# Layer 3 of a graph network on one core: two transfers of SyncE change places in each period

## The chip, the core and the metric

The kernel runs on one NeuronCore of a Trainium2 chip. Its engines work side by side, each on its own queue of instructions in the order in which they were written: PE (TensorE, matmuls; its weight loads are shown as PEld), DVE (VectorE), ACT (ScalarE), POOL (GpSimd) and SP (SyncE, which here only issues DMA transfers; ACT issues a few as well). Engines wait for one another by semaphores. The metric is the device time of one execution in microseconds (us): 2101.37 us for the kernel before, the median of three runs from 2099.18 to 2102.93.

## The reference, cut to what is computed

Four graph layers follow one another, each on `x + layer(relu(layernorm(x)))` with x of 32 graphs x 512 nodes x 64 features and one 512 x 512 adjacency matrix. The change lies in layer 3, a graph attention with 8 heads and then an output attention:

```python
def gat_layer(x, graph, W, b):
    h = x @ W
    s = jnp.einsum('bnd,bmd->bnm', h, h) * graph
    s = jnp.where(s == 0.0, NEG_INF, s)
    a = jax.nn.softmax(s, axis=2)
    return jnp.einsum('bnm,bmd->bnd', a, h) + b
heads = jax.vmap(lambda W, b: gat_layer(flow_x, graph, W, b))(Wh, bh)
...
x = jax.nn.leaky_relu(cat, negative_slope=0.01)
out = gat_layer(x, graph, W_out, b_out)
return jax.nn.leaky_relu(out, negative_slope=0.01)
```

Each softmax needs a maximum and a sum for every row of scores. Since the scores are symmetric, the kernel works on the transposed matrix: the maximum that it finds along one partition has to be subtracted along a column, so it must reach all partitions.

## The kernel before

Layers 0 to 2 take the first 450 us or so. Layer 3 then runs as 144 units: 128 pairs of attention heads (class `Heads`, L474) and 16 output attentions for two graphs each (class `Out`, L585). A unit has four row blocks r = 0 to 3 of 128 rows (C = 4), and each block holds two 512-column halves. A unit goes through these steps:

- `scores(r)`, L365: PE, two matmuls a block into a PSUM tile `s_ps`. That pool has two buffers (L1260), and `e_ps` of `exps` comes from the same two.
- `maxima(r)`, L375: DVE, two custom instructions a block (L382); they take the scores with the mask into `p_att` and leave the row maxima in `top`.
- `spread_out()`, L387: DVE transposes `top` (L389), and SP writes it into a small DRAM tile `top_row` with four transfers of 1 KB (L392).
- `spread_in()`, L396: SP reads `top_row` back, broadcast to all partitions, into `topb`, 128 x 1024 values, 512 KB (L398). This is the "broadcast of the maxima's rows". It must wait until `top_row` has landed.
- `shift(r)`, L403: POOL subtracts `topb` from a block (L404).
- `exps(r)`, L409: ACT takes the exponential of a block (L413), for odd r into `e_ps`. `join(r)`, L415: DVE adds block r - 1 to odd block r (L416).
- `totals()`, L429: PE sums the rows (L434), and ACT copies the result to `tot` (L439).
- `totals_out()`, L441: the sums are brought into a narrow form, `parts`, by two transfers of 4 KB, one issued by SP and one by ACT (both L446). SP's is the "spreading transfer of the sums". It must wait for the copy `tot`.
- `recips()`, L450: DVE adds the two parts (L452) and inverts them (L455). `recips_out()`, L457, and `recips_in()`, L463: SP sends them through DRAM (L459, L466) to `recb`.
- `values(j)`, L418: PE multiplies with the features (L422). `normalize()`, L470: DVE multiplies with `recb` (L472).
- `y_pe` (L549), `y_act` (L559) and `y_dve` (L568) of `Heads`: PE, ACT (L563) and DVE (L571) make the head's output `cat`. `Out` has `y_act` (L638), `back`, `back_dve`, `back_pool` and `store` (L641 to L663) in their place.

The order is written by hand. `planned` (L703) returns `period(t)`, and the loop at the end of layer 3 calls it once for each t. In period t, `now` is unit t, `ahead` is unit t + 1, and `unit(k)` is unit t - k. So one period works on several units at once: maxima of unit t, shifts and exponentials of unit t - 1, sums and values of unit t - 2, normalizing of unit t - 3, and the head output of unit t - 4. All five engines are under a manual schedule, so that each engine's instructions stand in its queue exactly as the calls in `period` follow one another. Two orders matter below:

- on ACT: `exps(0)` of unit t - 1, then `y_act` of unit t - 4, then `exps(2)`, the copy `tot` of unit t - 2, ACT's transfer of the sums, `exps(1)` and `exps(3)`;
- on SP: `recips_in` of unit t - 3, the four transfers of `spread_out` and the broadcast of `spread_in` (unit t), then SP's transfer of the sums (unit t - 2), `recips_out` (unit t - 2) and, where unit t - 5 is an `Out`, `store`.

PSUM tiles of the pool `ps_m` have two buffers (L1261) shared by `y_ps`, `tot_ps`, `back_ps` and a few others: in an ordinary period `totals` takes the buffer that the first half of `y_dve` has just read.

Of the kernel before, what the change touches and what calls it, by code (L numbers as in the profile page):

```python
# [22 lines left out]
def fast_form(  # L23
# [645 lines left out]
    def any_zero():  # L669

        def across(src, rows, name):
            ps = ps_m.tile([P, P], F32, name=name, tag="m")
            n = src.shape[0]
            nc.tensor.transpose(ps[:rows, :n], src, ident[:n, :n])
            return ps[:rows, :n]

        own = tiny.tile([P, 1], F32, name="own")
        nc.vector.tensor_reduce(own, least, AX.X, OP.min)
        two = tiny.tile([1, 2], F32, name="two")
        nc.vector.tensor_reduce(two[:, 0:1], across(own, 1, "own_ps"), AX.X, OP.min)  # L680
        best = tiny.tile([B // 2, 2], F32, name="best")
        nc.vector.tensor_reduce(
            best,
            across(least_out, B // 2, "out_ps").rearrange("b (k f) -> b k f", k=2),
            AX.X, OP.max,
        )
        worst = tiny.tile([B // 2, 1], F32, name="worst")
        nc.vector.tensor_reduce(worst, best, AX.X, OP.min)
        nc.vector.tensor_reduce(
            two[:, 1:2], across(worst, 1, "worst_ps"), AX.X, OP.min  # L690
        )
        flag = tiny.tile([1, 1], F32, name="flag")
        nc.vector.tensor_reduce(flag, two, AX.X, OP.min)
        nc.vector.scalar_tensor_tensor(
            again, flag, 0.0, unsound, op0=OP.is_equal, op1=OP.max
        )
# [6 lines left out]
    def planned(units, products):  # L703

        class Nothing:
            def __getattr__(self, name):
                return lambda *args: None

        nothing = Nothing()

        def period(t):
            def unit(lag):
                return units[t - lag] if 0 <= t - lag < len(units) else nothing

            now, ahead = unit(0), unit(-1)
            for r in range(2, C):
                now.scores(r)
            unit(3).recips_in()
            unit(4).y_pe()
            unit(1).shift(0)  # L720
            unit(1).exps(0)
            unit(4).y_act()
            u, h = products.get(t - 1, (None, 0))
            if u and h == H - 1:
                u.keep_product()
            unit(1).shift(2)
            unit(1).exps(2)
            for r in range(2, C):
                now.maxima(r)
            now.spread_out()  # L730
            now.spread_in()
            for r in range(2):
                ahead.scores(r)
            unit(4).y_dve()
            unit(3).normalize()
            for r in range(2):
                ahead.maxima(r)
            unit(4).back()
            unit(2).totals()
            unit(2).totals_out()  # L740
            unit(1).shift(1)
            unit(1).exps(1)
            u, h = products.get(t, (None, 0))
            if u:
                u.product(h)
            for j in range(C):
                unit(2).values(j)
            unit(1).join(1)
            unit(1).shift(3)
            unit(1).exps(3)  # L750
            unit(5).back_pool()
            unit(-2).make_gs()
            unit(2).recips()
            unit(2).recips_out()
            unit(5).store()
            unit(4).back_dve()
            unit(1).join(3)
            unit(-3).features(3)
            unit(-2).judge_product()
            unit(1).make_v()  # L760
            unit(-4).make_hx()
            unit(-2).make_g()
            for step in range(3):
                for lag, odd in ((step - 7, 0), (step - 11, 1)):
                    u = unit(lag)
                    if getattr(u, "i", None) == 0 and u.b % 2 == odd:
                        u.features(step)
            if t == len(units):
                any_zero()

        return period
# [1067 lines left out]
```

## Time and profile before

| What | before |
|---|---|
| runs (median, lowest, highest) | 2101.37, 2099.18, 2102.93 us |
| profiled execution: own time / span of its profile | 2099.58 / 2097.8 us |
| busy in the span: PE, DVE, ACT, POOL | 2002.6, 1786.2, 1227.9, 1432.7 us |
| starts of the copies `tot` (L439), first and last of 144 | 484.4 and 2075.8 us |
| mean distance of two such copies | 11.13 us |
| SP's issue: broadcast L398 / sums L446 | 0.35 / 0.57 us each |

The profile's page gives busy times of each engine, the costliest groups of instructions and what ended the idle time before them. The other views used are the waits (who waited for whom: us in total, times, longest), and the timeline of a window, in which each row is: start and length in us, engine, line, operation, tiles written and read, and in brackets the engine's idle time before it and what ended that. SPq and ACTq are transfers issued from the sequencers of SP and ACT; the length of such a row is the time that the issuing takes and not the flight of the data. The packet records of the trace give each DMA packet's start, length, size and queue; packets of SP's transfers are on queue 1, of ACT's on queue 10. The distance from one copy `tot` to the next is used as the length of a period.

### The profile page before, as it was taken

What the parts mean: (1) busy time and instruction counts of PE and PEld (TensorE: products, weight loads), DVE (VectorE), ACT (ScalarE), POOL (GpSimd) and SP (SyncE); (2) the same over time, 40 slices, a digit from 0 to 9 for tenths busy, and PEclk for the clock granted to TensorE, in tenths of its full rate; (3) what the DMA queues carried; (4) which work ended last, traced back from release to release, by engine and by line L of the source; (5) the groups of instructions that cost most, each with busy time, mean ns of one, the idle gap of its engine ahead of it and who ended that gap; (6) DMA issues with size and microseconds to landing.
All of it is one profiled execution on the core that took longest, in us unless ns stands there. A gap on an engine that the chain in (4) does not pass through costs nothing. (4 is left out here: it accounts for less than half of the span.)

```text
span 2097.8 us, 33009 instructions
## 1 busy us (share of the span) xinstructions
PE 2002.6 (95%) x11038; PEld 813.8 (39%) x11038; DVE 1786.2 (85%) x4257; ACT 1227.9 (59%) x1944; POOL 1432.7 (68%) x697
## 2 busy tenths in 40 slices
PE   7999999988999999999999999999999999999995
PEld 4667676652333333333333333333333333333321
DVE  6699997667998989898989898989888888988983
ACT  3444443335666666666666666666666666766553
POOL 3000000018898889888888988888888888888995
PEclk9999999989999999999999999999999999999998
DMA  5000000001222222222222222222222222222222
GB/s 139 1 1 2 1 2 1 1 22 57 77 75 69 78 77 73 78 76 82 68 78 77 72 77 77 77 71 74 68 77 73 77 67 73 77 71 74 77 68 78
DMA packets 135780, 129.35 MB, mean 62 GB/s; under 512 B 92792, under 2 KB 98080, under 8 KB 135472
## 3 DMA queue, kind: packets, MB, share of 16 engines
q1 hardware_dynamic: 116368, 126.35, 19.8%
q10 hardware_dynamic: 18720, 0.59, 0.5%
q8 instruction: 89, 1.46, 0.3%
q0 software_dynamic: 512, 0.20, 0.1%
q14 instruction: 91, 0.75, 0.1%
HBM read 119.48 MB, written 5.37 MB: 60 GB/s over the span
## 5 line engine op out<-in xcount | busy, mean ns | idle before, releaser
L404 POOL TENSOR_TENSOR p_att<-p_att,topb 128x1024 f32<-128x1024 f32 x576 | 1347.4, 2374 | 232.7 <-DMA topb<-top_row 130.6
L382 DVE CUSTOM_DVE_ANT_0 p_att<-s_ps,flow_neg 128x512 f32<-128x512 f32 x1152 | 727.8, 685 | 53.6 <-PE s_ps L370 51.9
L370 PE MATMUL s_ps<-hx,g 64*128 64x512 f32 x2048 | 545.3, 615 | 34.3 <-DVE p_att L416 24.6
L413 ACT ACTIVATE e_ps<-p_att 128x1024 f32<-128x1024 f32 x288 | 295.8, 1028 | 174.2 <-DVE top L382 107.8
L413 ACT ACTIVATE p_att<-p_att 128x1024 f32<-128x1024 f32 x288 | 304.2, 1056 | 149.6 <-POOL p_att L404 146.6
L416 DVE TENSOR_TENSOR p_att<-e_ps,p_att 128x1024 f32<-128x1024 f32 x288 | 346.5, 1203 | 24.7 <-ACT e_ps L413 24.4
L370 PEld LDWEIGHTS s_ps<-hx,g 64*128 64x128 f32 x2048 | 179.4, 186 | 343.1 <-DVE top L382 163.2
L422 PE MATMUL av<-p_att,hd 128*64 128x512 f32 x1024 | 264.3, 593 | 2.2 <-DVE o_att L472 2.0
L422 PE MATMUL av<-p_att,hn 128*64 128x512 f32 x1024 | 263.7, 592 | 0.0
L1053 POOL TENSOR_TENSOR x<-x,bias_b 128x512 f32<-128x512 f32 x16 | 20.3, 1271 | 280.0 <-DVE hn L826 280.0
L571 DVE SCALAR_TENSOR_TENSOR cat<-y_ps,bh,cat 128x512 f32<-128x512 f32 x256 | 178.1, 737 | 6.2 <-ACT cat L563 3.4
L563 ACT ACTIVATE cat<-y_ps,bh 128x512 f32<-128x512 f32 x256 | 161.7, 680 | 11.8 <-PE y_ps L553 8.7
L434 PE MATMUL tot_ps<-p_att,ones 128*32 128x512 f32 x1152 | 154.8, 610 | 1.6 <-DVE cat L571 0.5
L553 PE MATMUL y_ps<-o_att,wh_sb 64*128 64x512 f32 x512 | 143.2, 589 | 0.0
L598 PE MATMUL gT_ps<-cat,wo_sb 128*64 128x512 f32 x512 | 138.1, 618 | 0.0
L439 ACT COPY tot<-tot_ps 128x512 f32<-128x512 f32 x144 | 84.4, 586 | 85.0 <-PE tot_ps L434 83.6
L422 PEld LDWEIGHTS av<-p_att,hd 128*64 128x64 f32 x1024 | 73.2, 137 | 152.2 <-issue 141.2
L422 PEld LDWEIGHTS av<-p_att,hn 128*64 128x64 f32 x1024 | 74.8, 137 | 144.9 <-issue 144.9
L472 DVE TENSOR_TENSOR o_att<-av,recb 128x512 f32<-128x512 f32 x144 | 98.3, 683 | 34.9 <-DMA recb<-rec_row 34.6
L547 ACT COPY g<-g_ps 128x512 f32<-128x512 f32 x128 | 70.3, 588 | 95.3 <-PE g_ps L535 95.3
L977 PE MATMUL acc<-v,s 64*128 64x65 f32 x2048 | 124.1, 280 | 0.7 <-DVE s L963 0.4
L977 PEld LDWEIGHTS acc<-v,s 64*128 64x128 f32 x2048 | 121.2, 195 | 5.9 <-DVE o L993 1.2
(181 smaller groups left out, 2028.2 us busy)
## 6 DMA issues: line engine op xcount, KB each, us to landing
topb<-top_row SPq DMA_DIRECT2D x144, 512.0 KB
recb<-rec_row SPq DMA_DIRECT2D x288, 128.0 KB
top_row<-top_t SPq DMA_DIRECT2D x576, 1.0 KB
out_dram<-y SPq DMA_DIRECT2D x32, 128.0 KB
x<-in_x_dram SPq DMA_DIRECT2D x3, 1024.0 KB
parts<-tot ACTq DMA_DIRECT2D x144, 4.0 KB
parts<-tot SPq DMA_DIRECT2D x144, 4.0 KB
rec_row<-rec_flow SPq DMA_DIRECT2D x144, 4.0 KB
```

Source lines behind the costliest of these rows:

```text
L370: nc.tensor.matmul(ps[:, k], lhsT=g[halves(k), r * P : (r + 1) * P], rhs=x[halves(k), :], start=True, stop=True,)
L382: nc.vector.tensor_tensor_reduce(out=self.p[r][:, k], in0=ps[:, k], in1=flow_neg[:, r], scale=-1.0, scalar=BIG, op0=OP.add, op1=OP.min, ac ...
L404: nc.gpsimd.tensor_tensor(self.p[r], self.p[r], self.topb, OP.subtract)
L413: nc.scalar.activation(to, self.p[r], AF.Exp, scale=-1.0)
L416: nc.vector.tensor_tensor(self.p[r], self.joined, self.p[r - 1], OP.add)
L422: nc.tensor.matmul(self.av[halves(k), :], lhsT=self.v(k, j) if j % 2 else self.less_next(k, j), rhs=self.p[j][:, k], start=(j == 0), stop= ...
L434: nc.tensor.matmul(ps[q : q + 32, :], lhsT=ones, rhs=self.p[2 * e + 1][:, k], start=True, stop=True,)
L553: nc.tensor.matmul(ps, lhsT=wh_sb[halves(k), 2 * self.i + k, :], rhs=self.o[halves(k), :], start=True, stop=True,)
L563: nc.scalar.activation(self.cat[:, k], self.y[k], AF.Identity, bias=bh01[:, h : h + 1], scale=0.01)
L571: nc.vector.scalar_tensor_tensor(self.cat[:, k], self.y[k], bh[:, h : h + 1], self.cat[:, k], op0=OP.add, op1=OP.max,)
L598: nc.tensor.matmul(self.gps[halves(k), :], lhsT=wo_sb[:, h, :], rhs=Heads.cat.pop((self.b + k, h)), start=(h == 0), stop=(h == H - 1),)
L977: nc.tensor.matmul(self.acc[k][:, r], lhsT=self.s[b // 2][halves(k), b % 2, r * P : (r + 1) * P], rhs=self.v[halves(k), b], start=(b == 0) ...
```

## The change

In `period`, the call `now.spread_in()` moves from directly behind `now.spread_out()` to behind `unit(2).totals_out()`. Only SP's queue changes: in each period the broadcast L398 of unit t now stands behind SP's transfer of the sums L446 of unit t - 2, and no longer ahead of it. The instructions of PE, DVE, ACT and POOL are the same in the same order, and nothing is added or removed.

```diff
             for r in range(2, C):
                 now.maxima(r)
             now.spread_out()
-            now.spread_in()
             for r in range(2):
                 ahead.scores(r)
             unit(4).y_dve()
...
             unit(4).back()
             unit(2).totals()
             unit(2).totals_out()
+            now.spread_in()
             unit(1).shift(1)
             unit(1).exps(1)
```

## The prediction

> **What bounds the kernel now.** I read the page first, for which engines are full. PE is busy for 95% of the span, DVE for 85%; POOL's largest group, the shifts L404, has 232.7 us of idle time before it, ended mostly by the broadcast.
>
> ```profile
> PE 2002.6 (95%) x11038; PEld 813.8 (39%) x11038; DVE 1786.2 (85%) x4257; ACT 1227.9 (59%) x1944; POOL 1432.7 (68%) x697
> ...
> L404 POOL TENSOR_TENSOR p_att<-p_att,topb 128x1024 f32<-128x1024 f32 x576 | 1347.4, 2374 | 232.7 <-DMA topb<-top_row 130.6
> ```
>
> Then the waits in layer 3 (480 to 2080 us), those that touch the two transfers:
>
> ```profile
> POOL p_att L404 <- DMA topb<-top_row: 130.6, 88, 3.4
> ...
> PEld tot_ps L434 <- DVE cat L571: 100.7, 128, 1.1
> ...
> DVE rec_flow L452 <- DMA parts<-tot: 77.1, 118, 2.4
> ...
> DVE cat L571 <- ACT cat L563: 3.4, 14, 0.5
> ```
>
> DVE loses 77.1 us waiting for the sums; that is what the change can give. POOL already waits for the broadcast, so a later one reaches POOL at once. The sums on PE wait for `y_dve` (L571) nearly every period, while `y_dve` hardly waits for `y_act` (L563). The same waits for SP's own queue:
>
> ```profile
> SPq L398 <- DMA top_row<-top_t: 129.8, 220, 2.4
> SPq L446 <- ACT tot L439: 13.0, 15, 3.9
> ```
>
> Last, one ordinary period in the timeline:
>
> ```profile
> 1015.49 0.59 ACT L439 COPY tot<-tot_ps 128x512 f32<-128x512 f32 x1 [0.75 <-PE tot_ps L434]
> ...
> 1015.86 0.35 SPq L398 DMA_DIRECT2D topb<-top_row  x1
> ...
> 1016.10 0.50 ACTq L446 DMA_DIRECT2D parts<-tot  x1
> ...
> 1016.30 0.57 SPq L446 DMA_DIRECT2D parts<-tot  x1
> ...
> 1019.61 0.17 DVE L452 TENSOR_REDUCE rec_flow<-parts 128x8 f32<-128x16 f32 x1 [0.61 <-DMA parts<-tot]
> ...
> 1019.86 9.36 POOL L404 TENSOR_TENSOR p_att<-p_att,topb 128x1024 f32<-128x1024 f32 x4 [1.54 <-DVE rec_flow L452]
> ...
> 1019.93 1.18 DVE L416 TENSOR_TENSOR p_att<-e_ps,p_att 128x1024 f32<-128x1024 f32 x1
> ...
> 1022.26 1.06 ACT L413 ACTIVATE p_att<-p_att 128x1024 f32<-128x1024 f32 x1 [1.18 <-POOL p_att L404]
> ...
> 1023.26 1.27 ACT L563 ACTIVATE cat<-y_ps,bh 128x512 f32<-128x512 f32 x2
> ...
> 1024.13 0.21 DVE L389 STREAM_TRANSPOSE top_t<-top 128x32 f32<-128x32 f32 x1
> ...
> 1024.26 1.37 DVE L571 SCALAR_TENSOR_TENSOR cat<-y_ps,bh,cat 128x512 f32<-128x512 f32 x2
> ...
> 1024.37 1.31 SPq L392 DMA_DIRECT2D top_row<-top_t  x4
> ...
> 1025.21 1.06 PE L434 MATMUL tot_ps<-p_att,ones 128*32 128x512 f32 x8
> ...
> 1026.34 0.59 ACT L439 COPY tot<-tot_ps 128x512 f32<-128x512 f32 x1 [0.69 <-PE tot_ps L434]
> ...
> 1026.69 0.35 SPq L398 DMA_DIRECT2D topb<-top_row  x1
> ...
> 1027.13 0.58 SPq L446 DMA_DIRECT2D parts<-tot  x1
> ```
>
> The reader is to see two things. The broadcast is issued at 1026.69, ahead of the copy's end at 1026.93: today it hangs on the transpose at 1024.13 alone. And a chain runs from it through ACT's queue: broadcast, first shift, `exps(0)`, `y_act`, `y_dve`, sums, copy. POOL's wait at 1019.86 is put down to DVE, but that instruction had no use for `rec_flow`: the broadcast's last packet ended at 1019.10. The period is now set by a ring of PE and DVE (maxima, `y_dve`, sums, values, next scores), in which `y_dve` starts 0.13 us after the transpose begins.
>
> **What the Trainium skill says.** "DMA: Bandwidth & Descriptors", section "Anatomy of one DMA", says that a DMA's semaphore wait is made by the issuing sequencer before dispatch, not by the DMA engines. The trace agrees: SP's waits above are SP's own, and a waiting transfer holds those behind it. The same page, "Queues, rings and completion order", says that an engine takes the descriptors of one ring in order and goes round between rings. The trace fits: ACT's packets of the sums, behind no SP instruction, still ran only 2.3 to 2.7 us after the copy's end in this period, and 1.18 to 1.59 us after it in the one near 2022 us in which no broadcast was in flight; SP's there followed to 1.97 us.
>
> **The change part by part.**
>
> 1. Sums earlier. SP can issue them 0.02 us after the copy ends (so in the 15 places where it waited for it) and not 0.20 later, and their packets no longer follow the broadcast's: last packet about 1.97 us after the copy, usable about 0.4 us later (from packet end to L452 in most periods), 2.4 in all against 3.5 (1019.61 less 1016.08). That takes away the whole DVE wait, 77.1 us over 144 units, 0.53 a unit. What is late next is PE: DVE also waits 50.8 us for scores, and in over half of the periods the first maximum starts a constant 0.48 us after the modelled end of its score matmul, so PE sets it. Bounds of the gain: 0 to 77 us; I take 0 because step 3 sets the period anyway.
>
> 2. Broadcast later. Its new issue is the copy's end + 0.02 + 0.57 (issue of the sums) + 0.09 (SP's gap between two issues, 1016.21 to 1016.30) = copy's end + 0.69, or 1016.77 in place of 1015.86: 0.9 later. The four small transfers, still ahead of both, have then landed. Behind it on SP stands `recips_out`, which needs DVE's result some 2.4 us after the copy: not delayed. ACT's half of the sums isn't moved.
>
> 3. A new ring. The copy now gates the broadcast, and the broadcast gates, through ACT's order, the next copy. Going round once:
>    - issue to first shift: 4.00 here; mean 3.9 over the units
>    - first shift to `exps(0)`: 1022.26 - 1019.86 = 2.40
>    - `exps(0)` to `y_act`: 1.00 here, 0.96 in the periods where ACT runs through
>    - first half of `y_act` (page mean 0.68) and hand-over 0.04: 0.72
>    - `y_dve` to the copy: 1026.34 - 1024.26 = 2.08
>    - copy 0.59, then 0.69 to the broadcast's issue
>
>    Sum 3.9 + 2.40 + 0.96 + 0.72 + 2.08 + 0.59 + 0.69 = 11.34 us. No period can be shorter.
>
>    One term isn't shown by the trace: the flight of a broadcast right behind the sums. Its packets would start 0.97 us after issue, 1.66 after the copy, but the sums hold the rings till 1.97: at most +0.3. Below, -0.1, since the sums no longer mix into its tail. I take +0.1: 11.44.
>
>    The distances between the starts of the copies in the timeline: 143, together 1591.3 us. Four are under 10.35 (two of these in the drain at the end, left out), 21 near 10.50, 34 near 10.85, 57 near 11.15, 27 above 11.3. With 11.44: 2 x 1.17 + 21 x 0.94 + 34 x 0.59 + 57 x 0.29 = 2.3 + 19.7 + 20.1 + 16.5 = 58.6. The long periods have other causes (units of `Out`, feature making on ACT and PE) and don't grow; I take 5 us off, an estimate, for long ones that shrink since the sums come early. That leaves +54.
>
>    What hid this cost so far: `y_act` ended about 0.3 us before `y_dve` could start, and the broadcast didn't hang on the copy. 0.9 of delay goes through that cover in the first period.
>
> 4. A two-period path besides: broadcast, four shifts, `exps(3)`, `join(3)`, next maxima. Its slack (before `exps(3)` and `join(3)`) is 0.95 us on average, the delay 0.9: about nothing, and not added.
>
> Sum: the profiled execution, 2099.6 us (span 2097.8), + 54 = 2154; the median before is 1.8 higher, which I leave within the rounding.
>
> **The rivals.**
>
> - *Absorbed.* If `y_act` could take the delay (the trace shows only 14 waits of `y_dve` for it, 3.4 us), the slack of step 4 would cover the rest: 2101. Against it: 0.9 exceeds the 0.3 that the timeline shows. It would hold if the ring came to 11.0 or less.
> - *Faster.* The early sums let `join(3)` go earlier, the next maxima with it, and where PE isn't the limit the period shrinks. 77 us is the most; with PE tied in over half of the periods and Out periods gaining little, some 20: 2081. It decides if the ring is under about 10.8, so that the broadcast is never waited for. For it: the wait is real and in 118 periods. Against: POOL already waits for today's earlier broadcast.
> - *Dearer.* The flight takes its full +0.3 (11.64: 2 x 1.37 + 21 x 1.14 + 34 x 0.79 + 57 x 0.49 = 81), or the late `exps(3)` pushes the feature instructions behind it on ACT and so the next `exps(0)`: 2181 to 2200.
>
> That the order on SP changes as said is plain from the queues of both kernels: only SP's differs.
>
> **How the numbers follow.** The new ring 0.70 (2136 to 2175: flight -0.1 gives 2 x 0.97 + 21 x 0.74 + 34 x 0.39 + 57 x 0.09 = 36), dearer 0.13, absorbed 0.08, faster 0.09. The range reaches half-way into the neighbours: 2116 to 2186. Against a bound of 0.2% (4 us, about what this measurement can tell from no change): slower 0.83, same 0.08, faster 0.09.
>
> **What would show it.** The copy-to-copy distance near 11.4 with few below 11.2; the broadcast always issued about 0.7 us after the copy ends; waits of DVE for the sums nearly gone; waits of `y_dve` (L571) for `y_act` (L563) in most periods, not 14; PE's and ACT's waits for POOL up. The prediction is wrong if `y_dve` still starts straight behind the transpose, or if the flight of the broadcast falls well under 3.5 us because it no longer shares the rings.

## The result and the profile after

The changed kernel takes 2162.38 us (median of four runs, 2160.53 to 2166.83) against 2102.15 us for the kernel before (four runs, 2099.18 to 2103.18). The ratio is 1.0292, with a 95% interval from 1.0273 to 1.0311: slower by 60 us, where the forecast was 54 us and a time of 2154 us. The profiled execution took 2161.70 us, its span is 2159.8 us and so 62.0 longer than the span before.

The page, its busy times and the group of the shifts:

```profile
PE 2006.3 (93%) x11038; PEld 816.5 (38%) x11038; DVE 1792.9 (83%) x4257; ACT 1233.2 (57%) x1944; POOL 1432.0 (66%) x697
...
L404 POOL TENSOR_TENSOR p_att<-p_att,topb 128x1024 f32<-128x1024 f32 x576 | 1346.7, 2372 | 296.6 <-DMA topb<-top_row 127.1
```

No engine does more work: the largest difference of a busy time is 6.7 us, on DVE. The idle time ahead of POOL's shifts grew from 232.7 to 296.6 us. (The broadcast is named for less than half of it, 127.1 us; more of it than before is put down to PE, 72.3 us to its matmul L535 for one, whose result the shifts have no use for.) So the time went into waiting, and the waits of layer 3 say where (who waited for whom, us in total, times, longest; from 480 to 2140 us):

```profile
ACT p_att L413 <- POOL p_att L404: 233.5, 150, 3.6
...
PEld tot_ps L434 <- DVE cat L571: 170.6, 128, 2.1
...
POOL p_att L404 <- DMA topb<-top_row: 127.1, 66, 4.2
...
DVE p_att L416 <- ACT e_ps L413: 84.3, 134, 4.9
...
DVE cat L571 <- ACT cat L563: 82.1, 121, 1.4
...
PE tot_ps L434 <- DVE cat L571: 64.6, 116, 1.2
...
DVE rec_flow L452 <- DMA parts<-tot: 1.8, 4, 0.7
```

Read it from the last line up. The wait for the sums, 77.1 us before, is down to 1.8 us: the change did what it set out to do. In its place `y_dve` (L571) now waits for `y_act` (L563) in 121 periods, not in 14, and the weight loads of PE's sums (L434) wait 70 us longer for `y_dve`. The gain of one wait is more than paid by others further up the same chain.

SP's own waits show the cause. Before, the view had 220 waits of the broadcast for `top_row` (it counts each instruction of SP that waits, and a broadcast has several), and 15 of the sums for the copy. Now:

```profile
SPq L446 <- ACT tot L439: 268.9, 143, 6.4
...
SPq L398 <- DMA top_row<-top_t: 0.2, 1, 0.2
```

SP's sums wait for the copy 143 times in 144 units, and the broadcast behind it all but never waits for its own data (once, 0.2 us): when its turn comes, `top_row` has landed. One turn in the timeline (rows of ACT's, DVE's and PE's other work left out):

```profile
1027.10 0.59 SPq L398 DMA_DIRECT2D topb<-top_row  x1
...
1029.26 0.16 DVE L452 TENSOR_REDUCE rec_flow<-parts 128x8 f32<-128x16 f32 x1
...
1031.02 9.35 POOL L404 TENSOR_TENSOR p_att<-p_att,topb 128x1024 f32<-128x1024 f32 x4 [0.75 <-DMA topb<-top_row]
...
1033.41 1.06 ACT L413 ACTIVATE p_att<-p_att 128x1024 f32<-128x1024 f32 x1 [2.15 <-POOL p_att L404]
...
1034.37 1.25 ACT L563 ACTIVATE cat<-y_ps,bh 128x512 f32<-128x512 f32 x2
...
1034.42 0.21 DVE L389 STREAM_TRANSPOSE top_t<-top 128x32 f32<-128x32 f32 x1
...
1035.08 1.41 DVE L571 SCALAR_TENSOR_TENSOR cat<-y_ps,bh,cat 128x512 f32<-128x512 f32 x2 [0.45 <-ACT cat L563]
...
1037.01 0.59 ACT L439 COPY tot<-tot_ps 128x512 f32<-128x512 f32 x1 [0.22 <-PE tot_ps L434]
...
1037.62 0.57 SPq L446 DMA_DIRECT2D parts<-tot  x1
...
1038.42 0.59 SPq L398 DMA_DIRECT2D topb<-top_row  x1
```

Follow it down; the rows L452 and L389 aren't in the chain, and of the others each starts when the one above it lets it. Broadcast to first shift 3.92 us, first shift to `exps(0)` 2.39, to `y_act` 0.96, to `y_dve` 0.71, to the copy 1.93, to SP's sums 0.61, and 0.80 more to the next broadcast: 11.32 us, one whole period without slack. DVE stood idle for 0.45 us in it, waiting for the chain to come round. The transpose at 1034.42 was over at 1034.63, yet `y_dve` started only at 1035.08. `top_row` was issued at 1034.66, and the broadcast of the same rows 3.76 us later.

The distances of the copies `tot` (L439) are 1656.2 us in sum, 11.58 on average, against 1591.3 and 11.13: +64.8 us. Of the 143, 106 lie between 11.3 and 11.7, 27 at 11.7 or above, 9 between 11.0 and 11.3, and one, in the drain at the end, at 10.27. Before, 116 of them lay under 11.3. Taken period by period, the 116 short ones grew by 71.4 us together, whether they had been 10.5 (now 11.46 on average), 10.85 (11.53) or 11.15 us (11.54), and the 27 long ones shrank by 6.6. A floor has come in, and what was under it has been lifted to it.

### The profile page after: what moved, and what is told of

It reads as the page before. It is cut to its first block, busy times and chain, and to the rows that moved or that the text cites. A ratio compares the mean times of both kernels' runs of the same rounds, so it can differ in the third digit from the quotient of the medians.

```text
span 2159.8 us, 32847 instructions
## 1 busy us (share of the span) xinstructions
PE 2006.3 (93%) x11038; PEld 816.5 (38%) x11038; DVE 1792.9 (83%) x4257; ACT 1233.2 (57%) x1944; POOL 1432.0 (66%) x697
## 4 chain that ended last, share of the span: by engine, by line
PE 37%; POOL 18%; DMA 15%; ACT 13%; DVE 9%; issue 5%; SPq 3%; POOLq 0%; ACTq 0%; DVEq 0%
POOL p_att L404 17%; DMA topb<-top_row 14%; PE nt_ps L884 7%; PE av L422 7%; PE acc L977 6%; ACT p_att L413 5%; PE tot_ps L434 5%; DVE cat L571 3%; ACT cat L563 3%; DVE p_att L382 2%; ACT tot L439 2%; PE s_ps L370 2%; PE g_ps L535 2%; SPq L446 2%; PE gT_ps L598 2%
## 5 line engine op out<-in xcount | busy, mean ns | idle before, releaser
L404 POOL TENSOR_TENSOR p_att<-p_att,topb 128x1024 f32<-128x1024 f32 x576 | 1346.7, 2372 | 296.6 <-DMA topb<-top_row 127.1
L416 DVE TENSOR_TENSOR p_att<-e_ps,p_att 128x1024 f32<-128x1024 f32 x288 | 352.1, 1223 | 92.5 <-ACT e_ps L413 92.2
L571 DVE SCALAR_TENSOR_TENSOR cat<-y_ps,bh,cat 128x512 f32<-128x512 f32 x256 | 180.1, 745 | 82.1 <-ACT cat L563 82.1
L434 PE MATMUL tot_ps<-p_att,ones 128*32 128x512 f32 x1152 | 156.0, 614 | 65.1 <-DVE cat L571 64.6
L563 ACT ACTIVATE cat<-y_ps,bh 128x512 f32<-128x512 f32 x256 | 159.6, 673 | 0.0
L422 PEld LDWEIGHTS av<-p_att,hn 128*64 128x64 f32 x1024 | 73.8, 137 | 146.0 <-issue 146.0
L884 PE MATMUL nt_ps<-adj_t,hn 128*128 128x512 f32 x256 | 117.0, 600 | 0.8 <-DVE hn L848 0.8
```

Of the source, the lines that this page charges most:

```text
L404: nc.gpsimd.tensor_tensor(self.p[r], self.p[r], self.topb, OP.subtract)
L416: nc.vector.tensor_tensor(self.p[r], self.joined, self.p[r - 1], OP.add)
L422: nc.tensor.matmul(self.av[halves(k), :], lhsT=self.v(k, j) if j % 2 else self.less_next(k, j), rhs=self.p[j][:, k], start=(j == 0), stop= ...
L434: nc.tensor.matmul(ps[q : q + 32, :], lhsT=ones, rhs=self.p[2 * e + 1][:, k], start=True, stop=True,)
L563: nc.scalar.activation(self.cat[:, k], self.y[k], AF.Identity, bias=bh01[:, h : h + 1], scale=0.01)
L571: nc.vector.scalar_tensor_tensor(self.cat[:, k], self.y[k], bh[:, h : h + 1], self.cat[:, k], op0=OP.add, op1=OP.max,)
```

## The experiments

The theory: the copy now gates the broadcast on SP, the broadcast gates the copy one period later through POOL, ACT, DVE and PE, and the ring's length is the floor of the period. The rivals: the later broadcast is dear by itself, wherever the ring is cut; or the new order on SP's queue is dear by itself; or the sums' transfers are the matter. In the diffs the lines are those of `period`. The kernel before was measured anew beside each group of experiments (2101.16, 2104.02 and 2103.61 us); each ratio is to that median.

### Cutting the ring on ACT, in both kernels

In the ring `y_act` stands behind `exps(0)`, which needs the first shift. Putting `y_act` ahead cuts it there, without touching SP's queue.

```diff
             unit(1).shift(0)
-            unit(1).exps(0)
             unit(4).y_act()
+            unit(1).exps(0)
```

In the changed kernel:

> The changed kernel, and on ACT y_act of the head output stands ahead of exps(0), so the ring broadcast - first shift - exps(0) - y_act - y_dve - sums - copy - broadcast is cut at ACT while SP's order stays as changed. Ring theory: the next path is the one over two periods (broadcast, four shifts, exps(3), join(3), maxima, y_dve, sums, copy), some 22.2 us or 11.1 a period, so about 2105 us (2095 to 2120), and the waits of y_dve (L571) for y_act are gone. Rival, the late broadcast hurts through the four shifts and join(3), or through its longer flight, and not through y_act: stays at 2150 or above.

Measured: 2126.96 us (2126.53 to 2128.35), ratio 1.0126 (1.0109 to 1.0143). 35 of the 60 us are gone with SP's order as changed and the broadcast as tied to the copy as before. The rival that the order or the late broadcast is dear by itself falls for the larger part. Late exponentials aren't what the 35 us were either: DVE's joins (L416) wait for ACT even longer here, 156.2 us in 231 waits, than in the changed kernel, 84.3 us in 134. But the level that I expected is missed by over 20 us. Its wait of `y_dve` for `y_act` is gone altogether; what stands in the timeline instead (SP's, POOL's and ACT's rows):

```profile
1017.91 0.59 SPq L398 DMA_DIRECT2D topb<-top_row  x1
...
1021.94 9.35 POOL L404 TENSOR_TENSOR p_att<-p_att,topb 128x1024 f32<-128x1024 f32 x4 [1.05 <-PE s_ps L370]
...
1026.65 1.06 ACT L413 ACTIVATE p_att<-p_att 128x1024 f32<-128x1024 f32 x1 [0.39 <-POOL p_att L404]
1027.62 0.57 ACT L439 COPY tot<-tot_ps 128x512 f32<-128x512 f32 x1
...
1028.21 0.56 SPq L446 DMA_DIRECT2D parts<-tot  x1
...
1029.00 0.60 SPq L398 DMA_DIRECT2D topb<-top_row  x1
```

(The shift at 1021.94 is put down to PE, but it has no use for `s_ps`; it starts 4.03 us after the broadcast's issue, where the median of this run is 4.12.) PE's sums began at 1026.12 and ended at 1027.19 in this period, and yet the copy starts only when `exps(2)` is through: `exps(2)` stands ahead of the copy on ACT, and it waits for the second shift. That is a second ring: broadcast to shift 4.03, two shifts to `exps(2)` 4.71, to the copy 0.97, to the sums 0.59, to the broadcast 0.79: 11.09 us in this period. Over the whole run the medians of these links add up to 11.20; in 101 of 144 periods the copy starts within 0.1 us of the end of `exps(2)`, and 92 of the 143 distances of the copies lie between 11.0 and 11.3. The changed kernel has this ring too, some 0.3 us shorter than the first and so not seen. The prediction had missed it.

The same edit in the kernel before, as a control:

> The kernel before with the same move of y_act on ACT, as a control. Ring theory: there is no ring in the kernel before, y_dve hardly waits for y_act, so the move by itself gives little: 2090 to 2103 us. Rival, the move is worth tens of us by itself, so that the run of the changed kernel with it would tell nothing of a ring: under 2075.

Measured: 2102.11 us (2099.77 to 2103.80), ratio 1.0001 (0.9991 to 1.0011). The move on ACT is worth nothing where this ring isn't closed, so what it recovered in the changed kernel is the ring's.

### Cutting the second ring as well

`exps(2)` also moves behind the copy. The diff is against the changed kernel with the first move in it:

```diff
             unit(4).y_act()
             unit(1).exps(0)
...
-            unit(1).exps(2)
...
             now.spread_in()
+            unit(1).exps(2)
```

> The changed kernel with y_act ahead of exps(0) (as in the first run, which left 1.3%), and exps(2) behind the copy and ACT's transfer of the sums, so that no exponential of the unit that waits for the broadcast stands ahead of the copy on ACT. Ring theory: the second ring (broadcast, two shifts, exps(2), copy, broadcast, some 11.3 us) is cut as well; what is left is the two-period path of about 11.1 us: 2108 us (2098 to 2118). Rival, the rest of the loss comes by the four shifts, exps(3) and join(3) and not by ACT's order: 2122 or above.

Measured: 2118.68 us (2116.81 to 2120.48), ratio 1.0068 (1.0048 to 1.0087). The excess over the kernel before falls from 26 to 15 us, as it should if the second ring set the time. This second move wasn't run in the kernel before, so that its gain is the ring's rests on the trace of the run before it. The time is just outside the expected range. What remains may be step 4's path over `exps(3)` and `join(3)`: DVE's joins (L416) wait 143.8 us for ACT here, against 16.7 in the kernel before. That is argued, not shown, since delaying `exps(2)` itself also makes later exponentials late.

### Lengthening the ring

The counter-test: an ACT copy of 128 x 512 values into a tile that nobody reads, placed in the ring of the changed kernel. It only adds work.

```diff
+        def extra(self):
+            t = wk.tile([P, N], F32, name="extra", bufs=1)
+            nc.scalar.copy(t, urow)
...
             unit(1).exps(0)
+            unit(1).extra()
             unit(4).y_act()
```

> The changed kernel with one added copy of 128x512 (0.59 us, into an unused tile) on ACT between exps(0) and y_act. Ring theory: every period is one turn of the ring, so each grows by nearly the whole copy, 0.55 us: 2162 + 143 x 0.55 = 2241 us (2225 to 2255). Rival, the two-period path over exps(3) and join(3) sets the time, and y_dve has 0.45 us of cover before it: at most 0.14 a period, 2182 or below.

Measured: 2238.04 us (2233.91 to 2238.78), ratio 1.0635 (1.0618 to 1.0653). That is 75.7 us over the changed kernel (72 by the two ratios), 0.50 to 0.53 us in each of 143 periods for an instruction of 0.59, on an engine that is busy for 57% of the changed kernel's span. In the trace the link from `exps(0)` to `y_act` has grown from 0.96 to 1.47 us, and no other by more than 0.03; the ring adds up to 12.05, and the median period is 12.06. The waits of this kernel, lines shifted by four:

```profile
PEld tot_ps L438 <- DVE cat L575: 243.8, 128, 2.9
...
DVE cat L575 <- ACT cat L567: 154.3, 121, 2.2
```

`y_dve` waits for `y_act` 72 us longer than in the changed kernel, in the same 121 periods: the added copy is passed on nearly whole at this very place. Of all runs this one speaks most plainly for the ring.

### The late broadcast without the early sums

To part the two halves of the change, the broadcast was tied to the copy in the kernel before while the sums stayed behind it. A transfer of the copy into an unused tile stands ahead of the broadcast as a gate, once as small as it can be (32 bytes from one partition), once in the form of the sums' own.

```diff
+        def gate(self):
+            t = tiny.tile([P, 8], F32, name="gate")
+            nc.sync.dma_start(t[0:1, :], self.tot[0:1, 0:8])
...
             now.spread_out()
-            now.spread_in()
...
             unit(2).totals()
+            unit(2).gate()
+            now.spread_in()
             unit(2).totals_out()
```

> The kernel before with SP's order broadcast - sums kept, but one small transfer of 32 bytes of the copy into an unused tile stands ahead of the broadcast, so that the broadcast hangs on the copy without the sums being early. Ring theory: the ring is closed, but shorter by the cheaper issue (about 0.3 in place of 0.57 us) and by the packets of the sums that no longer stand ahead: about 11.1 us against 11.5, so it binds the short periods alone: about 2115 us (2105 to 2130). Rival, hanging on the copy at all costs the whole: 2155 or above; rival, only the sums' place matters: 2102.

> As the small gate, but the gate is a transfer of the sums' own shape and cost into an unused tile; the sums themselves stay behind the broadcast. This is the late broadcast alone, without early sums. Ring theory: the ring is as long as in the changed kernel (11.5 us), so about 2162 us (2152 to 2172), and DVE's waits for the sums are back without costing more. Rival, the early sums are what costs: about 2102.

Measured: 2197.03 us (ratio 1.0453, 1.0435 to 1.0472) with the small one and 2195.20 us (1.0444, 1.0424 to 1.0463) with the full one. Both expectations are missed. The small gate was to bring the broadcast nearly to where it was, but its issue costs more than the large one's. SP's queue with the small gate:

```profile
1014.97 0.71 SPq L443 DMA_DIRECT2D gate<-tot  x1
...
1015.92 0.42 SPq L398 DMA_DIRECT2D topb<-top_row  x1
...
1016.40 0.59 SPq L450 DMA_DIRECT2D parts<-tot  x1
```

So the broadcast came 0.97 us after the copy's end, with the full gate 0.83, and the two kernels were no pair at all. Both also push the sums to about 1.5 us after the copy, and this has a price that I hadn't foreseen. The full gate's wait of DVE for the sums:

```profile
DVE rec_flow L457 <- DMA parts<-tot: 203.6, 140, 2.5
```

203.6 us, against 77.1 before and 1.8 after. With the full gate the broadcast leaves as late as in the changed kernel (0.82). The sums are later and there is one more transfer, so 2195.20 less 2162.38 = 33 us is about what early sums are worth once the broadcast is late. It isn't the ring of the changed kernel that sets the time here: `y_dve` waits for `y_act` 13.0 us in 44 waits, not 82.1 in 121. The trace points to another closed chain: copy, late sums, reciprocals, `join(3)` behind them on DVE, next maxima, `y_dve`, copy. In all 128 head periods DVE waits at the reciprocals, and from there to `y_dve` it stands idle for 0.19 us only (median; 1.54 in the changed kernel). Copy to reciprocals 5.08, to `y_dve` 4.52, to the next copy 1.99: together 11.59, and the median of these periods is 11.58. No run cut or lengthened this chain. So the gates show that the broadcast's late place is dear without early sums too, but not how dear it is by itself.

### The sums off SP's queue

If the sums' place on SP was all there was to gain, ACT can issue both of its halves in the kernel before, and the broadcast stays early.

```diff
-            for e, queue in enumerate((nc.sync, nc.scalar)):
+            for e, queue in enumerate((nc.scalar, nc.scalar)):
```

> The kernel before, with both transfers of the sums issued by ACT and none by SP: the broadcast keeps its early place and doesn't hang on the copy, and the sums wait for nothing of SP. Ring theory: no ring, so not slower; the sums' packets still meet the broadcast's on the DMA engines, so DVE's wait for them stays near 77 us and little is gained: 2095 to 2106 us. Rival, SP's issue order by itself holds the sums up: DVE's wait goes and the time falls to 2085 or below.

Measured: 2107.60 us (2104.65 to 2111.75) against 2104.02, ratio 1.0019 (1.0012 to 1.0027): no gain, rather a little loss. The expectation was wrong about the wait: DVE's wait for the sums fell from 77.1 to 15.6 us, as the rival had it, and the time didn't follow. But it isn't early sums that took the wait away: their last packet ran 3.1 us after the copy's end (median), against 3.2 before. ACT issues twice ahead of `exps(1)`, and DVE's joins wait 73.8 us for ACT, not 16.7; DVE may simply reach the sums later. So this doesn't show that early sums alone are worth nothing.

### The copy early in the period

If the copy comes early, SP's order should not matter. First only the sums were moved to the start of the period in the kernel before:

```diff
             unit(3).recips_in()
+            unit(2).totals()
+            unit(2).totals_out()
             unit(4).y_pe()
...
-            unit(2).totals()
-            unit(2).totals_out()
```

> The kernel before, with totals() and totals_out() moved to the start of the period, ahead of y_pe and spread_out: SP issues the sums ahead of the broadcast as in the changed kernel, but the copy is early and depends on neither y_act nor exps(0) of the period. Ring theory: the order on SP costs nothing without the ring, and PE loses its wait for y_dve at the sums: not slower than 2102, some 2060 (2020 to 2100). Rival, sums that stand ahead of the broadcast cost by themselves (issue time, packets ahead in the DMA rings): 2110 or above.

Measured: 2249.33 us (2247.79 to 2252.70), ratio 1.0686 (1.0666 to 1.0706), the worst of all and a plain miss. `y_act` now has the copy ahead of it as well as `exps(0)`, and `y_dve`, which hardly waited before, waits in every head period:

```profile
DVE cat L571 <- ACT cat L563: 256.9, 128, 2.3
```

It says nothing of SP. The second attempt put `y_act` ahead of `exps(0)`, gave `y_dve`, the first shift and the products a later place to make room, and came in two forms that differ only in SP's order. In the diff, the lines that the moved calls leave behind further down and the move of the products are left out:

```diff
             for r in range(2, C):
                 now.scores(r)
+            unit(2).totals()
             unit(3).recips_in()
             unit(4).y_pe()
-            unit(1).shift(0)
-            unit(1).exps(0)
             unit(4).y_act()
+            for r in range(2, C):
+                now.maxima(r)
+            now.spread_out()
+            unit(2).totals_out()
+            now.spread_in()
...
+            for r in (0, 2):
+                unit(1).shift(r)
+                unit(1).exps(r)
...
             for r in range(2):
                 ahead.maxima(r)
+            unit(4).y_dve()
```

That form has the sums ahead of the broadcast; in the other `totals_out` and `spread_in` are exchanged.

> Sums and copy early in the period as in the run before, and the cause of that run's failure mended: y_act now stands ahead of exps(0) on ACT, y_dve behind the maxima of the next unit on DVE, and the product behind the values on PE. SP issues as in the changed kernel: top_row, sums, broadcast. Ring theory: the copy depends on nothing that waits for the broadcast, so the sums ahead of it cost nothing (their issue fits into the wait for top_row to land): some 2060 us (2020 to 2100), and within 10 us of the run with the sums behind. Rival, sums ahead of the broadcast cost by themselves: slower than that run by 30 us or more.

> The same with SP's order of the kernel before: top_row, broadcast, sums. Ring theory: some 2060 us (2020 to 2100), within 10 us of the run with the sums ahead. Rival: faster than that run by 30 us or more.

Measured: 2164.07 us (1.0290, 1.0273 to 1.0308) with the sums ahead and 2175.03 us (1.0342, 1.0325 to 1.0360) with them behind. The level was missed by 100 us or more in both; why this restructured period takes 11.6 to 11.7 us isn't settled (with the sums ahead, POOL waits 252.9 us for the broadcast, and DVE 111 us for `recb`, 15.4 in the changed kernel). The difference between the two still tells something: here the order of the change is 11 us *better* than the other. In the form with the sums ahead, SP comes to the sums 1.96 us after the copy's end (median), so they don't wait for it, and their issue fills time in which the broadcast would wait for `top_row`: it leaves 2.9 us after the copy in both forms. In this period the order of the two transfers costs nothing by itself; in the changed kernel the first one has to wait, and there it costs.

No version tried beats the kernel before.

## Why the prediction was right, step by step

- **Sums earlier (step 1).** Right as to the wait, 77.1 to 1.8 us, and the last packet of the sums runs 1.97 us after the copy's end, as worked out. Taking 0 for the gain was right for the sum that was made, since the ring sets the period; but the early sums aren't worthless. Beside an equally late broadcast they are worth about 33 us.
- **Broadcast later (step 2).** Right in kind, a little small. It is issued at the copy's end + 0.82 us (median), not + 0.69: SP's gap between the two is 0.23, not 0.09. Behind the transpose it stands 4.02 us, against 2.36 before.
- **The ring (step 3).** This carried the prediction, and held. The terms as measured (medians over the periods): issue to first shift 4.10 (taken as 4.0), first shift to `exps(0)` 2.39 (2.40), to `y_act` 0.96 (0.96), half of it and hand-over 0.70 (0.72), `y_dve` to the copy's end 2.52 (2.67), to the issue 0.82 (0.69). Sum 11.5, with 11.44 foreseen and a median period of 11.54 measured. So three errors of about 0.1 us, two up and one down, in part cancel; that the sum came this close is partly luck. Over the 116 short periods it comes to 71.4 us where 58.6 was worked out for 114 of them; the long periods gave back 6.6, where 5 was taken, a figure that the prediction didn't work out: luck. Together +64.8 us from the first copy to the last, against +54; the span grew by 62.0.
- **Two-period path (step 4).** "About nothing, and not added" held for the changed kernel: DVE's joins do wait more often for ACT (134 times, not 16), yet the sum came out without it. The list was incomplete, though. A second ring over `exps(2)`, 11.1 to 11.2 us long, lay just below the first; it took the experiment to see it. Had the ring of step 3 come out shorter than that, the forecast would have failed there.
- **The rivals.** "Absorbed" needed a ring of 11.0 or less and "faster" one under 10.8; it is 11.5. "Faster" was right that the wait of 77.1 us would go, and wrong that this is time. "Dearer" wasn't reached, but the flight came half-way to it: issue to first shift grew by 0.2, from 3.9 to 4.1, where 0.1 was taken and 0.3 the most. It is all there before the first packet, which runs 1.23 us after the issue begins, 0.98 before; the issue itself takes 0.25 longer (0.60 and 0.35). The signs named came true: 106 of 143 distances between 11.3 and 11.7 and four below 11.2, waits of `y_dve` for `y_act` in 121 periods, ACT's waits for POOL up from 193 to 372 us. PE's waits for POOL, named as well, stayed small (2.6 and 4.6 us).

What the runs show and what they don't: that the loss comes from the ring is shown from both sides, by cutting it on ACT, with the same edit in the kernel before as a control, and by lengthening it. That some 15 us are left with both rings cut is measured, its cause only argued. What sets the period of the kernel before isn't settled: the prediction takes a ring of PE and DVE for it, but the chain over the sums and the reciprocals, which the full gate seems to close, is nearly closed there too (DVE waits for the sums in 112 of 128 head periods and then stands idle for 0.32 us up to `y_dve`).

## What to carry to other kernels

A transfer moved behind another on a queue that works in order takes over that one's wait. Before such a move, ask whether the data that the other waits for hangs, through the order of some other engine's queue and one period back, on the very transfer that is moved; if so, add up the way round and compare the sum with each period, not with their mean: every period shorter than the ring grows to it, and the longer ones stay. A wait that goes is worth nothing if the ring was the longer way, and once a ring is cut, look for the next one just below it.

## What the runs showed of the hardware that was not expected

- A smaller transfer isn't always quicker to issue: on SP 0.71 us for 32 bytes out of one partition, 0.57 us for the sums of 4 KB, both right behind the copy.
- The broadcast's issue takes 0.35 us when it stands behind the four transfers of `top_row`, and 0.60 us right behind the sums, 0.23 us after their issue has ended. Its 512 KB and 128 packets of 4096 bytes are the same in both. In the rearranged period with the sums ahead it follows their issue by 0.40 us, and takes 0.34. So the order alone doesn't make it longer; what does isn't shown.
- ACT's packets of the sums run 1.18 to 1.59 us after the copy's end in the changed kernel, and 2.3 to 2.8 us after it in the kernel before (medians), where SP's broadcast was in flight: a bulk transfer of one queue holds a small one of another for about 1.1 us. One packet of the broadcast takes 0.2 us in the trace, so that ACT's are held for longer than one of these; why isn't shown. (In the period near 2022 us that the prediction sets beside it, a broadcast was in flight as well, but its last packet ended 0.3 us before ACT's first.)
